# A graph layer's edge pass: 125-row gathers, columns in two groups of five, single rows on SyncE, the bias from node features in SBUF

## The chip, the cores and the metric

The kernel runs on one core of a Trainium2 chip. The core's engines are TensorE (PE: matmuls; PEld: its weight loads), VectorE (DVE), ScalarE (ACT), GpSimd (POOL) and SyncE (SP), which issues most of the plain transfers. Sixteen DMA engines move the data between HBM and the core's memory (SBUF, and PSUM for matmul results). The metric is device time in microseconds (us), as the median of several runs.

## The reference

One message-passing layer on 12500 nodes with 64 features each and 412500 edges (both directions of 200000 random edges, and a loop for every node), sorted by receiver. With `h = relu(layernorm(x))`, cut to what matters:

```python
msg_in = concat([h[src], h[dst], edge_attr], axis=-1)       # 412500 x 160
messages = swish(msg_in @ W1 + b1) @ W2 + b2                # 412500 x 64
att = softmax(swish(msg_in @ Wa1 + ba1) @ Wa2 + ba2, axis=0)  # over all edges
aggregated = segment_sum(messages * att, dst, 12500)
upd = concat([h, aggregated], axis=-1)
out = x + swish(upd @ Wu1 + bu1) @ Wu2 + bu2
```

Everything is float32.

## The kernel before, in words

**Tables by node.** The first layers of message and attention are linear in the three parts of `msg_in`. So a prologue normalizes the nodes and computes two tables of 128 numbers per node (64 for attention, 64 for messages): `ts_d` for senders and `tr_d` for receivers, both in HBM. The normalized features stay in SBUF, transposed, as `hT` (two nodes' 64 features stacked on 128 partitions, 49 x 128 columns), and go to HBM as `hT_d`, too.

**The edge pass.** Edges go in blocks of 125 (`EP`), eight blocks (`K`) to a group, 413 groups (`NG`). For each group `load(g)` starts two groups ahead (`AHEAD`):

- POOL gathers the senders' rows of `ts_d` by an indirect DMA per block (L513), 125 or 126 rows of 512 bytes into `gs`, from a pool of seven buffers (`gather`). Each block has 125 edges; with `WIDE` = 126 the blocks with odd j fetch a row more, into a partition that nobody reads.
- SP loads the receivers' windows of 32 rows (`wins`, L534, three buffers), and every fourth group (`NQ`) the edge features (`eo`, L524) and receivers' numbers (`dbs`, L527). DVE turns the numbers into a one-hot matrix (L538), and PE adds receivers' and edges' share in PSUM (`pe`, L542).

**Blocks by columns.** For some groups (`chosen`, before: every third) POOL gathers seven blocks only. For the eighth, SP loads the senders' numbers into `num` (L458) and DVE turns them into column numbers of `hT` (`places`, L467 to L473). ACT reads these into registers and copies one column at a time from `hT` to `cols` (L484), in six lots of up to 24 spread over three groups (`burst`, `SLOTS`). DVE masks the half that is meant (L547), and PE multiplies by the senders' weights into the same PSUM (L548).

**After the gather.** `begin(g)` adds gathered rows and PSUM on DVE (L553; a block by columns is copied, L555), and ACT takes the tanh (L556). `end(g)` forms messages and attention logits on DVE (L566 to L577). Softmax runs online, in batches of four groups. `by_node` (L620, L626), `project` (L637) and `put` (L651 to L658) sum the weighted messages by receiver into `sums` in SBUF, some groups behind.

**Tiles for the end.** The last stage needs two things by node tile: the update's bias, `h @ Wu1[:64] + bu1`, and `x + bu2`. They are made during groups 17 to 119, in 13 tiles (`NT`), and go to HBM (`bq_d`, `xb_d`). `node_bias` loads the features back from `hT_d` into `hb` (L329), sets a row of ones by a DVE memset (L327) and lets PE multiply by the weights with the bias as 65th row (L331); ACT copies the result (L348). `tile_rest` loads x into a buffer of the same pool (L366), adds `bu2` on DVE (L370) and stores (L371), all within one group.

**What sets the order.** The loop over g is written out by hand: `pin` keeps the order on an engine. Unpinned instructions (tile bias, DMAs) are placed by a scheduler. Each engine works its own instructions in order and waits on semaphores. DMAs of a kind take turns on eight semaphores: in the built program a DMA of SP (or a gather of POOL) waits for the landing of the eighth one before it.

Of the kernel before, what the change touches and what calls it, by code (L numbers as in the profile page):

```python
# [44 lines left out]
F32 = mybir.dt.float32  # L45
I32 = mybir.dt.int32
AF = mybir.ActivationFunctionType
ALU = mybir.AluOpType
AX = mybir.AxisListType
ENG = mybir.EngineType  # L50
# [3 lines left out]
P = 128  # L54
EP = 125
D = 64
DE = 32
U = 64
C = 2 * U
S1 = U + 1  # L60
K = 8
# [11 lines left out]

EVERY = 3
PHASE = 1
SLOTS = (((0, 24), (24, 24)), ((48, 24), (72, 12)), ((84, 24), (108, 17)))
ROUND = 12582912.0
WIDE = 126
EPS = 1e-5
# [4 lines left out]
PARTS = [("pair", 4 * C), ("we", C), ("bias", C), ("wu2h", 2 * D), ("wa2", U), ("bu2", D), ("w_bu", U),  # L84
         ("w2b", U), ("wu1a", U), ("wu2", D), ("ba2", 1)]
HALVED = 4
# [4 lines left out]
def gnn_kernel(ctx: ExitStack, tc: tile.TileContext, n_edges, x, src, src_row, dst, dst_row, first, edge,  # L91
# [33 lines left out]
    we, bias, wa2, bu2_r, ba2_c = (part[k] for k in ("we", "bias", "wa2", "bu2", "ba2"))  # L125
    w_bu = part["w_bu"][:D + 1]
    w2b = part["w2b"][:S1]
    wu1a, wu2 = part["wu1a"][:U], part["wu2"][:U]
# [206 lines left out]
def tile_bias(tc, c, first, v, work, ps, bus):  # L335

    nc = tc.nc
    m = min(NC, v["NB"] - c)
    if first:
        bus[c] = work.tile([U, P * NC], F32, name="bu", bufs=1)[:, :P * m]  # L340
    elif m <= 4:
        return
    i = 0 if first else 4
    n = min(4, m - i)
    pb = node_bias(tc, c + i, v, work, ps).rearrange("u b (h p) -> u h p b", h=2)
    to = bus[c].rearrange("u (h k p b) -> u k h p b", h=2, k=2, b=m // 2)
    for k in range(i // (m // 2), (i + n) // (m // 2)):
        nc.scalar.copy(to[:, k], pb[:, :, :, k * m // 2 - i:(k + 1) * m // 2 - i])  # L348
    if i + n == m:
        for h in range(2):  # L350
            nc.sync.dma_start(v["bq_d"][c // NC, h * U:(h + 1) * U, :P // 2 * m],
                              bus[c][:, h * P // 2 * m:(h + 1) * P // 2 * m])


def halves(ap, c, n, k, NB):

    return ap.rearrange("(h p b) d -> p h b d", h=2, b=NB)[:, :, c + k * n // 2:c + (k + 1) * n // 2, :]


def tile_rest(tc, c, v, work):  # L360

    nc = tc.nc
    n = min(NC, v["NB"] - c)
    xt = work.tile([P, 4, P], F32, name="hb").rearrange("p a b -> p (a b)")[:, :n * D]
    for k in range(2):
        nc.sync.dma_start(  # L366
            xt[k * P // 2:(k + 1) * P // 2].rearrange("p (h b d) -> p h b d", h=2, d=D),
            halves(v["x"], c, n, k, v["NB"]))
    xv = xt.rearrange("p (b d) -> p b d", d=D)
    nc.vector.tensor_tensor(xv, xv, v["bu2_r"][:, None, :].to_broadcast([P, n, D]), ALU.add)  # L370
    nc.sync.dma_start(v["xb_d"][c // NC, :, :n * D], xt)  # L371


def one_pass(tc, n_edges, v):
    nc = tc.nc
    NB, T, NG, NP, NT = (v[k] for k in ("NB", "T", "NG", "NP", "NT"))
    ident, iota_w, bj, dloc, src_full, base_sb, real, unreal, far, wrong = (
        v[k] for k in ("ident", "iota_w", "bj", "dloc", "src_full", "base_sb", "real", "unreal",
                       "far", "wrong"))
# [12 lines left out]
    with ExitStack() as ctx:  # L392
# [5 lines left out]
        stand = keep.tile([P, NH + 2 * W], F32, name="stand")  # L398
        base_lo = keep.tile([1, NG + 1], I32, name="base_lo")
        base_hi = keep.tile([1, NG + 1], I32, name="base_hi")  # L400
        nc.vector.memset(base_lo, 0)
# [34 lines left out]
        with tc.tile_pool(name="work2", bufs=2) as work2, \  # L436
                tc.tile_pool(name="small", bufs=3) as small, \
                tc.tile_pool(name="pre_ps", bufs=AHEAD + 1, space=PSUM) as pre_ps, \
                tc.tile_pool(name="one_ps", bufs=1, space=PSUM) as one_ps:
            pes, gss, lgs, ps_, psums, sps, pps, ees, mts, nums, cols = ({} for _ in range(11))  # L440

# [9 lines left out]

            chosen = {g for g in range(8, NG - 12) if g % EVERY == PHASE}

            def numbers(g):
                if g in chosen:
                    e = (g * K + K - 1) * EP
                    n = nums[g] = small.tile([P, EP], I32, name="num", bufs=2)
                    nc.sync.dma_start(n, bass.AP(tensor=v["src_row"].tensor,  # L458
                                                 offset=v["src_row"][:, e:].offset, ap=[[0, P], [1, EP]]))

            def places(g):
                if g not in chosen:
                    return
                n = nums[g]
                near = small.tile([1, EP], F32, name="near", bufs=1)
                to = small.tile([1, EP], I32, name="to", bufs=2)
                pin(nc.vector.tensor_scalar(to, n[0:1], 1, None, op0=ALU.logical_shift_right))  # L467
                m = NB // 2
                pin(nc.vector.tensor_scalar(near, to, 1.0 / m, 0.5 / m - 0.5, op0=ALU.mult, op1=ALU.add))
                pin(nc.vector.tensor_scalar(near, near, ROUND, None, op0=ALU.add))  # L470
                pin(nc.vector.tensor_scalar(near, near, ROUND, float(1 - m * P), op0=ALU.subtract, op1=ALU.mult))
                pin(nc.vector.scalar_tensor_tensor(to, to, float(P), near, op0=ALU.mult, op1=ALU.add))
                pin(nc.vector.tensor_scalar(n, n, 1, None, op0=ALU.bitwise_and))  # L473
                cols[g] = small.tile([P, EP], F32, name="cols", bufs=2), to

# [10 lines left out]
            def burst(g, k):  # L486
                for i in range(EVERY):
                    columns(g + 3 + i, *SLOTS[EVERY - 1 - i][k])

            at_sp, at_lo, at_hi, bus = {}, {}, {}, {}  # L490

# [12 lines left out]
            def load(g):  # L504

                t = g * K
                if g % NQ == 0:
                    registers(g, ENG.SP, at_sp)
                full = gather.tile([P, K, C], F32, name="gs")
                gs = gss[g] = full[:EP]  # L510
                for j in range(K - (g in chosen)):
                    rows = WIDE if j % 2 == 1 else EP
                    nc.gpsimd.indirect_dma_start(  # L513
                        out=full[:rows, j, :], out_offset=None, in_=ts_d[:, :],
                        in_offset=bass.IndirectOffsetOnAxis(ap=src_full[:rows, t + j:t + j + 1], axis=0))
                if g % NQ == 0:
# [16 lines left out]
                for r in range(2):  # L533
                    nc.sync.dma_start(win[r * R:(r + 1) * R, :, r, :],  # L534
                                      tr_w[bass.ds(at_sp[g], R), :, :])
                for h in range(2):
                    e = slice(h * E2 // 2, (h + 1) * E2 // 2)
                    pin(nc.vector.tensor_scalar(eo[:WR, e], db[:, e], bj[g // NQ % 2 * WR:(g // NQ % 2 + 1) * WR, g, h:h + 1], None,  # L538
                                                op0=ALU.is_equal))
# [10 lines left out]
            def begin(g):  # L550

                n = K - (g in chosen)
                pin(nc.vector.tensor_tensor(gss[g][:, :n, :], pes[g][:, :n, :], gss[g][:, :n, :], ALU.add))  # L553
                if n < K:
                    pin(nc.vector.tensor_copy(gss[g][:, n, :], pes[g][:, n, :]))  # L555
                pin(nc.scalar.activation(pes[g], gss[g], AF.Tanh))  # L556
# [161 lines left out]
            for g in range(NG):  # L718
# [18 lines left out]
                if g + AHEAD < NG:  # L737
                    load(g + AHEAD)
                numbers(g + EVERY + 4)
                places(g + EVERY + 3)  # L740
                if more:
# [20 lines left out]
                if g == min(40, NG):  # L762
                    pin(nc.vector.tensor_reduce(far[:, 1:2], dloc, AX.X, ALU.min, negate=True))
                if g == min(44, NG):

                    worst = small.tile([EP, 1], F32, name="worst", bufs=1)
                    pin(nc.vector.tensor_reduce(worst, far, AX.X, ALU.max))
                    worst_ps = one_ps.tile([P, 4, P], F32, name="mt")[:EP, 0, :EP]
                    pin(nc.tensor.transpose(worst_ps, worst.to_broadcast([EP, EP]), ident[:EP, :EP]))
                if g == min(45, NG):  # L770
                    pin(nc.vector.tensor_reduce(worst, worst_ps, AX.X, ALU.max))
                    pin(nc.vector.tensor_scalar(wrong, worst, 0.0, None, op0=ALU.is_gt))
                if g >= 16 and g // 8 - 2 < NT:
                    c = (g // 8 - 2) * NC
                    if g % 8 in (1, 5):
                        tile_bias(tc, c, g % 8 == 1, v, work2, one_ps, bus)
                    elif g % 8 == 3:
                        tile_rest(tc, c, v, work2)

# [273 lines left out]
def _laid_out(w):  # L1053
# [16 lines left out]
    part["ba2"][:] = w["ba2"]  # L1070
    part["w_bu"][:D + 1] = np.concatenate([w["Wu1"][:D], w["bu1"][None]])
    part["w2b"][:S1] = np.concatenate([w["W2"], w["b2"][None]])
    part["wu1a"][:U] = w["Wu1"][D:]
# [42 lines left out]
```

## Time and profile before

| | |
|---|---|
| median of 10 runs | 4599.79 us (4598.45 to 4601.67) |
| the profiled execution | 4599.87 us, span 4598.1 us |
| busy | POOL 3538.4 us, DVE 3355.3, PE 2388.4, ACT 2213.4 |
| gathers (L513) | 3173, first at 51.46 us, last at 4541.11 us |
| columns copied by ACT (L484) | 16375 |
| DMA, mean | 87 GB/s |

The profile is one execution, read on the core itself. The span reaches from the first to the last instruction; the profiled execution's own time has 1.8 us around it. A line of the groups reads: source line, engine, operation, tiles (out<-in), number of instructions | busy us, mean ns of one | idle us of the engine just before them, and what ended most of it. A line of the timeline reads: start, duration, engine, line, operation, and in brackets the idle time before it and what ended that. A line of the waits reads: who <- for whom: us in total, times, longest. A line of one source line reads: engine, operation, count, duration in ns (least, median, greatest), first and last start in us. A gather's duration on POOL is the time in which POOL issues it, not the time until its rows land. An engine name with q is its sequencer, which waits and issues DMAs.

### The profile page before, as it was taken

The numbers are of one execution on the slowest core, as the hardware profiler recorded it, in microseconds if no ns is written. First come the engines' busy times: TensorE is split into PE (matmuls) and PEld (weight loads), VectorE is DVE, ScalarE is ACT, GpSimd is POOL, SyncE is SP. The second block draws the span as 40 slices with busy tenths as digits, with TensorE's granted clock in tenths as the row PEclk, the third lists the DMA queues.
The fourth block names the chain that finished last, engine by engine and source line by source line (L and its number), as shares of the span: only waits on it lengthen the run. The fifth ranks groups of instructions, "written<-read, shape, count | busy, mean of one in ns | idle before, by whom it ended". The sixth has DMA issues, their size and how long they took to land. (4 is left out here: it accounts for less than half of the span.)

```text
span 4598.1 us, 81803 instructions
## 1 busy us (share of the span) xinstructions
PE 2388.4 (52%) x11509; PEld 1917.7 (42%) x11509; DVE 3355.3 (73%) x9768; ACT 2213.4 (48%) x17651; POOL 3538.4 (77%) x3198
## 2 busy tenths in 40 slices
PE   6455555555554554544555554555554555555455
PEld 4344444334444443434444444444443444444344
DVE  6767777777787776777777776777777777777777
ACT  3445545445554544544544444545545445445412
POOL 4777777777777777777777777777777777777775
PEclk8656666666666666566666655566666655556666
DMA  8333343343333333333333333333333333333333
GB/s 267 83 81 87 87 98 91 84 98 87 87 86 82 76 79 82 75 81 81 73 83 81 73 82 82 73 81 81 74 81 79 75 82 76 79 81 75 80 98 85
DMA packets 335625, 398.57 MB, mean 87 GB/s; under 512 B 170293, under 2 KB 266088, under 8 KB 334690
## 3 DMA queue, kind: packets, MB, share of 16 engines
q0 software_dynamic: 205168, 205.98, 19.5%
q1 hardware_dynamic: 128530, 177.64, 16.5%
q10 hardware_dynamic: 1376, 9.67, 0.5%
q14 instruction: 457, 3.74, 0.3%
q8 instruction: 94, 1.54, 0.1%
HBM read 365.34 MB, written 25.72 MB: 85 GB/s over the span
## 5 line engine op out<-in xcount | busy, mean ns | idle before, releaser
L513 POOL DMA_INDIRECT gs<-ts_d,src_sb x3173 | 3521.2, 1110 | 1018.5 <-issue 871.2
L542 PE MATMUL pe<-wins,eo 128*125 128x256 f32 x3304 | 1501.2, 630 | 1256.8 <-DVE eo L538 874.7
L484 ACT COPY cols<-hT 128x1 f32 x16375 | 1617.9, 187 | 749.0 <-issue 732.2
L542 PEld LDWEIGHTS pe<-wins,eo 128*125 128x125 f32 x3304 | 988.3, 316 | 1585.5 <-DVE eo L538 952.6
L553 DVE TENSOR_TENSOR gs<-pe,gs 125x1024 f32<-125x1024 f32 (+1 forms) x413 | 487.2, 1180 | 913.7 <-DMA gs<-ts_d,src_sb 878.4
L556 ACT ACTIVATE pe<-gs 125x1024 f32<-125x1024 f32 x413 | 424.1, 1027 | 1311.9 <-DVE gs L553 716.9
L620 DVE TENSOR_SCALAR wt<-iota_w,dloc,p 125x40 f32<-125x40 f32 x3304 | 749.4, 342 | 1.6
L626 PE MATMUL sp<-wt,acts 125*65 125x40 f32 x6608 | 634.3, 268 | 12.7 <-DVE wt L620 12.1
L626 PEld LDWEIGHTS sp<-wt,acts 125*65 125x65 f32 x6608 | 599.7, 184 | 18.2 <-DVE wt L620 16.7
L637 PEld LDWEIGHTS mt<-ss,w2u 65*128 65x128 f32 x826 | 211.6, 283 | 454.5 <-issue 359.2
L637 PE MATMUL mt<-ss,w2u 65*128 65x40 f32 x826 | 186.8, 320 | 367.1 <-DVE gm L603 358.8
L538 DVE TENSOR_SCALAR eo<-dbs,bj 64x250 f32<-64x250 int32 x826 | 300.7, 391 | 18.2 <-DMA dbs<-in_dst_row_dram 8.7
L596 PE MATMUL mt<-ident,mx 125*128 125x125 f32 x110 | 48.1, 437 | 507.5 <-DVE sums L655 430.7
L574 DVE TENSOR_TENSOR pe<-pe,w_all 125x512 f32<-125x512 f32 x413 | 288.7, 699 | 13.4
L572 DVE SCALAR_TENSOR_TENSOR pe<-pe,gs 125x512 f32<-125x512 f32 x413 | 286.7, 694 | 9.2
L566 DVE SCALAR_TENSOR_TENSOR acts<-pe,gs 125x512 f32<-125x512 f32 x413 | 283.3, 686 | 10.9 <-ACT pe L556 2.7
L577 DVE TENSOR_REDUCE lg<-pe 125x8 f32<-125x512 f32 x413 | 283.7, 687 | 9.4
L596 PEld LDWEIGHTS mt<-ident,mx 125*128 125x128 f32 x110 | 19.9, 181 | 518.9 <-issue 516.7
L658 DVE COPY stand<-nmax 64x40 f32 x826 | 183.5, 222 | 4.4
L655 DVE TENSOR_TENSOR sums<-sums,mt 64x40 f32 x606 | 114.3, 189 | 26.5 <-PE mt L637 21.1
L607 ACT ACTIVATE scale<-fall 128x1 f32<-128x1 f32 x110 | 22.2, 202 | 204.8 <-DVE fall L606 204.7
L651 DVE SCALAR_TENSOR_TENSOR sums<-sums,scale,mt 64x40 f32 x220 | 55.6, 253 | 72.4 <-PE mt L637 69.3
(125 smaller groups left out, 1102.1 us busy)
## 6 DMA issues: line engine op xcount, KB each, us to landing
eo<-in_edge_dram SPq DMA_DIRECT2D x103, 500.0 KB
dbs<-in_dst_row_dram SPq DMA_DIRECT2D x206, 250.0 KB
gs<-ts_d,src_sb POOLq DMA_INDIRECT x3173
wins<-tr_d SPq DMA_DIRECT2D x826, 32.0 KB
num<-in_src_row_dram SPq DMA_DIRECT2D x131, 62.5 KB
ts_d<-ts SPq DMA_DIRECT2D x5, 896.0 KB
tr_d<-tr ACTq DMA_DIRECT2D x5, 896.0 KB
hT_d<-hT ACTq DMA_DIRECT2D x1, 3136.0 KB
```

The source lines that it names most:

```text
L484: pin(nc.scalar.copy(to[:, first + i:first + i + 1], hT[:, bass.ds(regs[i], 1)]))
L513: nc.gpsimd.indirect_dma_start(out=full[:rows, j, :], out_offset=None, in_=ts_d[:, :], in_offset=bass.IndirectOffsetOnAxis(ap=src_full[:ro ...
L538: pin(nc.vector.tensor_scalar(eo[:WR, e], db[:, e], bj[g // NQ % 2 * WR:(g // NQ % 2 + 1) * WR, g, h:h + 1], None, op0=ALU.is_equal))
L542: pin(nc.tensor.matmul(pe[:, 2 * q:2 * q + 2, :], eo[:, q * EP:(q + 1) * EP], win[:, q // 2, :, :], start=True, stop=q < H - 1 or g not in ...
L553: pin(nc.vector.tensor_tensor(gss[g][:, :n, :], pes[g][:, :n, :], gss[g][:, :n, :], ALU.add))
L556: pin(nc.scalar.activation(pes[g], gss[g], AF.Tanh))
L572: pin(nc.vector.scalar_tensor_tensor(att, th[:, :, 0:U], 1.0, gs[:, :, 0:U], op0=ALU.add, op1=ALU.mult))
L574: pin(nc.vector.tensor_tensor(att, att, wa2[:EP, None, :].to_broadcast([EP, K, U]), ALU.mult))
L577: pin(nc.vector.tensor_reduce(lgs[s][:, k:k + K], att, AX.X, ALU.add))
L620: pin(nc.vector.tensor_scalar(wt[:, j, :], iota_w[:EP, j // H, :], dloc[:, g * K + j:g * K + j + 1], p[:, k + j:k + j + 1], op0=ALU.is_equ ...
L626: pin(nc.tensor.matmul(sp, acts[g % ACTS][:, j, :], wt[:, j, :], start=j == 0, stop=j == K - 1))
L637: pin(nc.tensor.matmul(pp, w2u.rearrange("s h u -> s (h u)"), sps.pop(g), start=True, stop=True))
```

## The change

- All gathers have 125 rows; `WIDE` goes.
- `chosen` takes two groups in five (g mod 5 = 1 or 4) instead of one in three. Their columns come in five lots of 24 (the last 29), at most one lot in each half of a group's pass.
- Every eighth group (8, 16, ... 408) leaves out one gather more. For this block SP reads the senders' numbers into registers and issues a transfer for each row of 512 bytes, 16 rows in each of the eight groups before it, into a tile of its own (`one_gs`); DVE adds the block by itself.
- The update's bias comes from `hT` in SBUF: PE multiplies two nodes' features at once by a weight matrix with two blocks (`w_bup`), and DVE adds `bu1` while it moves the result from PSUM. The loads of `hb` and the memset go. The instructions are pinned, and the store follows two groups later (`tile_bias_out`).
- `tile_rest` is split in three: x is asked for in one group, `bu2` is added three groups later, and the store follows three groups after that. x has a buffer of its own.

The core of the diff (`...` marks what is left out):

```diff
-EVERY = 3
-PHASE = 1
-SLOTS = (((0, 24), (24, 24)), ((48, 24), (72, 12)), ((84, 24), (108, 17)))
+LOTS = ((0, 24), (24, 24), (48, 24), (72, 24), (96, EP - 96))
+ROUNDS = 5
+SLOTS = {1: ((5, 1), (4, 0), (4, 1), (3, 0), (3, 1)), 4: ((5, 0), (5, 1), (4, 0), (4, 1), (3, 0))}
-WIDE = 126
+QUEUES = [(ENG.SP, 8, 0, 16)]
...
-    pb = node_bias(tc, c + i, v, work, ps).rearrange("u b (h p) -> u h p b", h=2)
+    pb = ps.tile([P, 4, P], F32, name="mt")[:, :n // 2, :]
+    pin(nc.tensor.matmul(pb, v["w_bup"], v["hT"][:, (c + i) // 2:(c + i + n) // 2, :], start=True, stop=True))
...
-        nc.scalar.copy(to[:, k], pb[:, :, :, k * m // 2 - i:(k + 1) * m // 2 - i])
...
+        pin(nc.vector.tensor_scalar(
+            to[:, k, :, :, at:at + 2 * q - 1:2],
+            pb[rows, (b - i) // 2:(b - i) // 2 + q, :].rearrange("u q (h p) -> u h p q", h=2),
+            v["bu1"][rows], None, op0=ALU.add))
...
-            chosen = {g for g in range(8, NG - 12) if g % EVERY == PHASE}
+            chosen = {g for g in range(8, NG - 12) if g % ROUNDS in SLOTS}
...
             def burst(g, k):
-                for i in range(EVERY):
-                    columns(g + 3 + i, *SLOTS[EVERY - 1 - i][k])
+                for i in (3, 4, 5):
+                    slots = SLOTS.get((g + i) % ROUNDS, ())
+                    if (i, k) in slots:
+                        columns(g + i, *LOTS[slots.index((i, k))])
...
+            def single(q, g):
+                if g < NG - 4:
+                    t = g * K + K - 1 - (g in chosen)
+                    rows_at[q, g] = small.tile([1, EP], I32, name=f"one_src{q}", bufs=2)
+                    nc.sync.dma_start(rows_at[q, g], v["src_row"][:, t * EP:(t + 1) * EP])
+            def rows(q, g):
...
+                loads, regs = nc.values_load_multi_w_load_instructions(
+                    rows_at[q, g][0:1, a:a + n], engines=[engine], min_val=0, max_val=NP - 1,
+                    skip_runtime_bounds_check_because=WHY)
+                for one in loads:
+                    pin(one)
+                for k in range(n):
+                    pin(dma[engine].dma_start(alone[g][a + k:a + k + 1, :], ts_d[bass.ds(regs[k], 1), :]))
...
-                for j in range(K - (g in chosen)):
-                    rows = WIDE if j % 2 == 1 else EP
+                for j in range(K - (g in chosen) - (g in alone)):
                     nc.gpsimd.indirect_dma_start(
-                        out=full[:rows, j, :], out_offset=None, in_=ts_d[:, :],
-                        in_offset=bass.IndirectOffsetOnAxis(ap=src_full[:rows, t + j:t + j + 1], axis=0))
+                        out=gs[:, j, :], out_offset=None, in_=ts_d[:, :],
+                        in_offset=bass.IndirectOffsetOnAxis(ap=src_sb[:, t + j:t + j + 1], axis=0))
...
+                for q in range(len(QUEUES)):
+                    if QUEUES[q][0] == ENG.SP:
+                        rows(q, g)
...
+                if g in alone:
+                    pin(nc.vector.tensor_tensor(gss[g][:, n, :], pes[g][:, n, :], alone.pop(g), ALU.add))
```

## The prediction

> **What bounds the kernel now.** I began with the page's busy shares and costliest groups. POOL is the busiest engine, at 77%, and one line is almost all of it.
>
> ```profile
> PE 2388.4 (52%) x11509; PEld 1917.7 (42%) x11509; DVE 3355.3 (73%) x9768; ACT 2213.4 (48%) x17651; POOL 3538.4 (77%) x3198
> ...
> L513 POOL DMA_INDIRECT gs<-ts_d,src_sb x3173 | 3521.2, 1110 | 1018.5 <-issue 871.2
> ```
>
> The reader is to see that POOL's missing 23% is no slack. 1018.5 us of idle time lie before the 3173 gathers; the waits put 871.2 us of it down to "issue" in 2859 pieces of at most 0.3 us, and 49.1 us to the start. That is 0.30 us before every gather, with nothing to wait for: a gather costs its duration plus 0.30. Second, the timeline of POOL in a middle stretch:
>
> ```profile
> 2061.14 1.27 POOL L513 DMA_INDIRECT gs<-ts_d,src_sb  x1 [0.30 <-issue]
> 2062.72 1.00 POOL L513 DMA_INDIRECT gs<-ts_d,src_sb  x1 [0.30 <-issue]
> 2064.02 1.21 POOL L513 DMA_INDIRECT gs<-ts_d,src_sb  x1 [0.31 <-issue]
> 2065.53 1.21 POOL L513 DMA_INDIRECT gs<-ts_d,src_sb  x1 [0.30 <-issue]
> 2067.04 0.99 POOL L513 DMA_INDIRECT gs<-ts_d,src_sb  x1 [0.30 <-issue]
> 2068.34 1.21 POOL L513 DMA_INDIRECT gs<-ts_d,src_sb  x1 [0.30 <-issue]
> 2069.86 1.00 POOL L513 DMA_INDIRECT gs<-ts_d,src_sb  x1 [0.30 <-DVE sums L655]
> ```
>
> There are two kinds of gather, 1.21 and 1.00 us, in turn, with two long ones side by side now and then. The code issues 125 rows for even j and 126 for odd j. A group with a column block stops at j = 6, so j = 6 and the next group's j = 0 stand together, both with 125 rows: that is the pair of long ones. The order from the first gather on fits everywhere: 1652 gathers of 125 rows start on average 1.517 us before their successor, 1520 of 126 rows (the last one has none) 1.305 us before theirs. 1652 x 1.517 + 1520 x 1.305 = 4489.7 us, which is the distance from the first gather (51.46) to the last one (4541.11). So POOL is the bound from end to end. Of the rest of the span, 51.5 us lie before it and 57.0 us after the last start.
>
> Third, the waits of DVE and of SP's queue, and the nearest thing to a one-row transfer that SP issues, by its line:
>
> ```profile
> DVE gs L553 <- DMA gs<-ts_d,src_sb: 878.4, 256, 18.4
> ...
> SPq L534 <- PE pe L542: 1238.0, 164, 14.3
> ...
> L180 SPq DMA_DIRECT2D base_sb<-in_first_dram x1: 307/307/307, 8.2 to 8.2; - x1
> L534 SPq DMA_DIRECT2D wins<-tr_d x826: 316/317/1672, 82.9 to 4496.2; - x166
> ```
>
> The consumers wait for gathers (878.4 us on DVE, 2.1 us in each of 413 groups of 4490/413 = 10.87 us), POOL hardly for them. While bias and x tiles are made (groups 17 to 119) DVE's add starts up to 27 us after a group's last gather, and even then POOL runs on, since it has seven buffers. SP mostly waits for PE to free a window buffer, so it is ahead.
>
> **The change part by part.**
>
> *125 rows in every gather.* The 126-row kind goes, and each gather that was one pays 1.517 - 1.305 = +0.212 us. The trace has the case of a 125-row gather behind another of 125 rows 131 times: 1.515 us. All after the change stand so; I take 1.517. The packet sizes on the gathers' queue say why: 46074 packets of 4096 bytes and 29554 of 512, which is 1652 x 15 + 1521 x 14 and 1652 x 5 + 1521 x 14. So 125 rows go out as 5 shares of 25 rows (three packets of 8 rows and one of 1), 126 as 14 shares of 9 (one of 8, one of 1). That ties the duration to the row count and not to a place in the group.
>
> *Fewer gathers.* Before, groups 8 to 400 with g mod 3 = 1 (131) have one block by columns. After, g mod 5 = 1 or 4 there: 157. In addition 51 groups (8, 16, ... 408) get one block as single rows. 3304 - 157 - 51 = 3096 gathers, 77 fewer.
>
> *The sum on POOL.* 3095 steps of 1.517 = 4695.1 us, and 2.8 us for the one long wait at the start (3.14 instead of 0.30 at 91 us), which stood in the other kind's mean: 4697.9, against 4489.7: +208.2. The last gather now has 125 rows: from its start to its landing the median is 3.40 us, against 2.66 for 126: +0.7 on the tail. Total +208.9. The profiled execution took 4599.87 us (1.77 more than its span; the median is 0.08 lower), so 4599.87 + 208.9 = 4808.8. Split: 77 fewer gathers at the old mean of 1.415 give -109; 3096 dearer ones at 1.517 - 1.415 give +316.
>
> The page DMA: Bandwidth & Descriptors of the Trainium skill, section Anatomy of one DMA, gives a fixed cost that scales with nothing plus bytes over a rate. By it, 125 and 126 rows should cost POOL nearly the same, the row count would drop out, and the sum would be 77 x 1.415 less, an estimate of 4491. The two kinds in the timeline, 0.21 us apart at under 1% of bytes, speak against it.
>
> *Columns in two groups of five.* ACT copies 157 x 125 = 19625 columns instead of 16375; 24 take 2.32 us in the timeline, so 3250 more cost 314 us. Lots stay 785 against 786, so their register loads stay. ACT goes from 2213 to about 2510 us in a longer span, 52%. A pass has at most 29 + 29 columns, 5.6 us, and about 1.2 us of register loads, in an 11.3 us group. DVE gets 26 more groups of L467 to L473 (1.58 us), L547 (0.34) and L555 (0.28), less 0.13 on L553: +54 us. PE 26 x 0.75. All is covered by POOL's 11.3 us per group; without that cover the 54 us on DVE would be the price.
>
> *Single rows on SyncE.* 51 x 125 = 6375 issues more on SP, each a register operation (0.037), a move (0.029) and the transfer. The shape is not in the trace; the nearest row is the one-row load at 0.307, bounds 0.3 and 0.58 (the longer L527 loads). So 0.374 each, 15.6 per group: 5.8 us, and 0.34 for the register load. SP's issues, moves and loads before come to 666 us, 1.6 per group: together 7.8 us of 11.3. Behind them on the queue wait the window, edge and receiver loads of the next group. Each transfer also waits for the landing of the eighth before it: eight issues are 3.0 us, window loads land in 1.94 (median), edge loads in 5.4, so some 2.4 us more every fourth group. SP may run over two groups ahead (three window buffers), some 22 us: the 6 us are hidden. DVE gets 51 more adds, about 0.28 (L555): 14 us. The rows are asked for in the eight groups before, so nobody should wait for them. Price on the path: 0; lower bound 0, since a shorter wait of the consumers does not speed POOL; upper bound in rival 2.
>
> *Bias from SBUF, x rows asked for earlier.* 50 loads of hb (0.606 us each on SP), 25 memsets (12.1 us on DVE) and 26 ACT copies (13.8 us) go. In their place DVE does 50 adds out of PSUM, 64x256, between L655 (0.19) and L574 (0.70); the nearest shape, L538, says 0.39: 20 us. DVE's waits on hb (50.6 + 28.1 us) go or shrink. All of that lay beside POOL, which never stopped there: 0. What is late next is the same gather as before. Net on DVE: 54 + 14 + 20 - 12 = +76 us, 3431 of 4807, 71%.
>
> **Rivals.** 1. *The long and the short kind follow something other than the row count*, odd j for instance, which the trace has only together with 126 rows. Then of the 3096 gathers 1464 stay short: 1632 x 1.517 + 1464 x 1.305 = 4386.3, 103 less than 4489.7: 4496, faster. For it: no 125-row gather with odd j exists before. Against: the packets, which differ as the row counts do. It decides against me if the mean step falls below 4490 / 3096 = 1.450, that is if over 31% of the gathers stay short.
>
> 2. *SP becomes the bound.* With 1.95 us of other work per group this needs (11.34 - 1.95) / 15.6 = 0.60 us per single row, or landings of more than 11.34 / (18 / 8) = 5 us. At 0.65 (the 0.58 row and its moves) a group takes 12.1 us; 400 of these with the 272 us around them: 5112. Against: 0.307 and 0.317 for small transfers, and landings of 1.94 us.
> [...]
>
> 3. *Consumers come late here and there*, for uneven groups of 6 to 8 gathers or rows on their way; POOL then runs out of buffers: 10 to 50 us more, 4820 to 4860. Against: it did not at 27 us of lag.
>
> **How the numbers follow.** My forecast 0.90, rival 1 0.04, rival 2 0.03, rival 3 0.03. 0.2% (9 us) is about what a measurement of this kernel can tell from no change. Slower: 0.90 + 0.03 + 0.03, less a little for something unnamed, 0.95; faster 0.04; same 0.01. The range starts at 4790, a step of 1.511, below any 125-row mean here, and reaches to 4860 to take in rival 3. Rivals 1 and 2 stay outside.
>
> **What would show it.** Right: POOL gathers x3096 of 1.21 us without short ones, 0.30 idle before each, and the last start near 4749. DVE's wait for gathers grows from 878 us, as 208 us of span bring only 76 of work. SP's single rows at about 0.31. Wrong: 1.00 us gathers among those of 125 rows; POOL waiting for DVE; DVE waiting for one_gs or wins at SP.

## The result, and the profile after

The changed kernel takes 4808.1 us (4806.5 to 4810.9), the kernel before 4599.7 us beside it: a ratio of 1.0454, 95% interval 1.0444 to 1.0463. It is slower by 208 us, and the forecast was 4809. The profiled execution took 4808.78 us with a span of 4807.1.

The page of the changed kernel, busy shares and the groups that answer to those shown of before:

```profile
PE 2482.8 (52%) x11561; PEld 1984.3 (41%) x11561; DVE 3514.6 (73%) x10052; ACT 2499.4 (52%) x20875; POOL 3769.7 (78%) x3121
...
L571 POOL DMA_INDIRECT gs<-ts_d,src_sb x3096 | 3752.5, 1212 | 996.7 <-issue 884.9
```

77 gathers fewer than before, and 231 us more of POOL's time in them, since the mean went from 1110 to 1212 ns. The timeline of POOL in the same middle stretch, and its last gather:

```profile
2060.23 1.21 POOL L571 DMA_INDIRECT gs<-ts_d,src_sb  x1 [0.30 <-issue]
2061.74 1.21 POOL L571 DMA_INDIRECT gs<-ts_d,src_sb  x1 [0.30 <-issue]
...
4750.38 1.21 POOL L571 DMA_INDIRECT gs<-ts_d,src_sb  x1 [0.30 <-issue]
```

The short gathers of 1.00 us are gone. Before each gather stand the same 0.30 us with nothing to wait for, so POOL sets the time from end to end, as before: (4750.4 - 51.6) / 3095 = 1.518 us per step. The waits of POOL, DVE and PE, and of SP's queue:

```profile
POOL gs L571 <- issue: 884.9, 2900, 0.3
DVE gs L614 <- DMA gs<-ts_d,src_sb: 851.6, 318, 7.3
DVE bu L357 <- PE mt L348: 120.2, 25, 10.2
PE pe L603 <- DMA wins<-tr_d: 116.8, 27, 11.2
DVE eo L599 <- DMA dbs<-in_dst_row_dram: 61.5, 7, 18.8
...
SPq L592 <- PE pe L603: 212.9, 109, 11.0
```

The wait of 1238.0 us on SP's queue, the sign that SP was ahead, has shrunk to 212.9: the single rows have eaten most of SP's lead, and PE and DVE now wait for window and receiver loads here and there. None of this reaches POOL: after its first gather it waits longer than 0.4 us only three times, all before 95 us, and 13 of its 3095 steps are over 1.7 us (3.22 at most), 11 of them in the first 1300 us.

### The profile page after: what moved, and what is told of

It is laid out like the page before. It is cut to its first block, busy times and chain, and to the rows that moved or that the text cites. A ratio compares the mean times of both kernels' runs of the same rounds, so it can differ in the third digit from the quotient of the medians.

```text
span 4807.1 us, 108404 instructions
## 1 busy us (share of the span) xinstructions
PE 2482.8 (52%) x11561; PEld 1984.3 (41%) x11561; DVE 3514.6 (73%) x10052; ACT 2499.4 (52%) x20875; POOL 3769.7 (78%) x3121
## 5 line engine op out<-in xcount | busy, mean ns | idle before, releaser
L571 POOL DMA_INDIRECT gs<-ts_d,src_sb x3096 | 3752.5, 1212 | 996.7 <-issue 884.9
L504 ACT COPY cols<-hT 128x1 f32 x19625 | 1922.2, 187 | 962.5 <-issue 931.4
L603 PE MATMUL pe<-wins,eo 128*125 128x256 f32 x3304 | 1547.4, 642 | 1468.5 <-DVE eo L599 1079.1
L614 DVE TENSOR_TENSOR gs<-pe,gs 125x1024 f32<-125x1024 f32 (+2 forms) x413 | 477.4, 1156 | 873.0 <-DMA gs<-ts_d,src_sb 851.6
L683 DVE TENSOR_SCALAR wt<-iota_w,dloc,p 125x40 f32<-125x40 f32 x3304 | 782.6, 367 | 1.2
L689 PE MATMUL sp<-wt,acts 125*65 125x40 f32 x6608 | 671.6, 275 | 11.1 <-DVE wt L683 10.3
L689 PEld LDWEIGHTS sp<-wt,acts 125*65 125x65 f32 x6608 | 631.9, 191 | 20.9 <-DVE wt L683 16.3
L599 DVE TENSOR_SCALAR eo<-dbs,bj 64x250 f32<-64x250 int32 x826 | 301.0, 394 | 70.8 <-DMA dbs<-in_dst_row_dram 61.5
L721 DVE COPY stand<-nmax 64x40 f32 x826 | 215.5, 261 | 3.2
L357 DVE TENSOR_SCALAR bu<-mt,w_all 64x256 f32<-64x256 f32 (+1 forms) x50 | 23.9, 478 | 120.6 <-PE mt L348 120.2
```

Source lines behind the costliest of these rows:

```text
L504: pin(nc.scalar.copy(to[:, first + i:first + i + 1], hT[:, bass.ds(regs[i], 1)]))
L571: nc.gpsimd.indirect_dma_start(out=gs[:, j, :], out_offset=None, in_=ts_d[:, :], in_offset=bass.IndirectOffsetOnAxis(ap=src_sb[:, t + j:t ...
L603: pin(nc.tensor.matmul(pe[:, 2 * q:2 * q + 2, :], eo[:, q * EP:(q + 1) * EP], win[:, q // 2, :, :], start=True, stop=q < H - 1 or g not in ...
L683: pin(nc.vector.tensor_scalar(wt[:, j, :], iota_w[:EP, j // H, :], dloc[:, g * K + j:g * K + j + 1], p[:, k + j:k + j + 1], op0=ALU.is_equ ...
L689: pin(nc.tensor.matmul(sp, acts[g % ACTS][:, j, :], wt[:, j, :], start=j == 0, stop=j == K - 1))
```

## The experiments

Each kernel was timed beside the kernel before on the same chip, in three rounds; a row of the table gives both. E1 to e4 ran together on another chip than the rest. On that one the kernel before itself took 5390 us instead of 4600, so those four are compared only with each other, and what set that chip apart is taken up at the end.

| run | rows per gather | columns | single rows | gathers | us | before beside it | ratio (95%) |
|---|---|---|---|---|---|---|---|
| before | 125, odd j 126 | 1 in 3 | no | 3173 | 4599.7 | | |
| after | 125 | 2 in 5 | yes | 3096 | 4808.1 | 4599.7 | 1.0454 (1.0444 to 1.0463) |
| e1 | 125 | 1 in 3 | no | 3173 | 4931.0 | 5390.1 | 0.9143 (0.9117 to 0.9170) |
| e2 | 125, even j 126 | 1 in 3 | no | 3173 | 5478.5 | 5390.1 | 1.0172 (1.0135 to 1.0210) |
| e3 | 125, odd j 126 | 2 in 5 | yes | 3096 | 6161.0 | 5390.1 | 1.1421 (1.1387 to 1.1455) |
| e4 | 125 | 2 in 5 | no | 3147 | 4892.7 | 5390.1 | 0.9071 (0.9045 to 0.9096) |
| e5 | as e3 | 2 in 5 | yes | 3096 | 4500.8 | 4598.2 | 0.9785 (0.9769 to 0.9801) |
| e6 | as e2 | 1 in 3 | no | 3173 | 4573.4 | 4598.2 | 0.9945 (0.9928 to 0.9961) |
| e7 | 126 | 2 in 5 | yes | 3096 | 4325.3 | 4598.2 | 0.9405 (0.9389 to 0.9420) |
| e8 | 128 | 2 in 5 | yes | 3096 | 4318.3 | 4598.2 | 0.9392 (0.9376 to 0.9407) |
| e9 | 128 | 2 in 5 | no | 3147 | 4052.8 | 4599.4 | 0.8812 (0.8797 to 0.8826) |
| e10 | 128 | 1 in 3 | no | 3173 | 4087.3 | 4599.4 | 0.8887 (0.8872 to 0.8902) |
| e11 | 128 | 1 in 5 | no | 3226 | 4147.6 | 4599.4 | 0.9018 (0.9003 to 0.9033) |
| e12 | 128 | 1 in 2 | no | 3108 | 4467.4 | 4598.9 | 0.9715 (0.9699 to 0.9732) |

In e4 and e9 to e12 the eighth block of groups 8, 16, ... is gathered again instead of read as single rows; all kernels compute the whole layer.

### Row count alone and each part alone, first try (e1 to e4)

My theory: the row count sets a gather's time, and the rest of the change is worth its 77 gathers. The rivals: the place in the group (odd or even j) sets it; or the single rows on SP cost something.

```diff
 # e1 and e2, in the kernel before
-                    rows = WIDE if j % 2 == 1 else EP
+                    rows = EP                              # e1
+                    rows = WIDE if j % 2 == 0 else EP      # e2
 # e3, in the changed kernel
-                gs = gss[g] = gather.tile([P, K, C], F32, name="gs")[:EP]
+                full = gather.tile([P, K, C], F32, name="gs")
+                gs = gss[g] = full[:EP]
...
+                    wide = 126 if j % 2 == 1 else EP
-                        out=gs[:, j, :], out_offset=None, in_=ts_d[:, :],
-                        in_offset=bass.IndirectOffsetOnAxis(ap=src_sb[:, t + j:t + j + 1], axis=0))
+                        out=full[:wide, j, :], out_offset=None, in_=ts_d[:, :],
+                        in_offset=bass.IndirectOffsetOnAxis(ap=v["src_full"][:wide, t + j:t + j + 1], axis=0))
 # e4, in the changed kernel
-QUEUES = [(ENG.SP, 8, 0, 16)]
+QUEUES = []
```

> The kernel before with 125 rows in every gather; nothing else changes. Theory (the row count sets POOL's step, and POOL is the bound): 3172 steps of 1.517 us instead of 1652 of 1.517 and 1520 of 1.305, so 4600 + 1520 x 0.212 = about 4922 us, and no gather of 1.00 us is left. Rival 1 (the place in the group, odd j, sets it): the 1.00 us gathers stay where j is odd, time unchanged at 4600.

> The kernel before with 126 rows at even j and 125 at odd j, the other way round. Theory (row count): 1652 gathers are now short and 1520 long, 131 more short ones than before: 4600 - 131 x 0.212 = about 4572 us, and the gathers at even j show 1.00 us. Rival 1 (odd j is short whatever its rows): odd j stays at 1.00 us and even j at 1.21, time unchanged at 4600.

> The changed kernel with one part undone: 126 rows at odd j again. Theory (the row count is all of the loss, and the rest of the change is worth its 77 fewer gathers): 1632 steps of 1.517 and 1463 of 1.305, so 4808 - 1463 x 0.213 = about 4497 us, 2.2% under the kernel before. Rival 3 (the single rows or the uneven groups hold the consumers up once POOL is quicker): above 4520 us, with POOL waiting for buffers.

> The changed kernel without single rows on SyncE: POOL gathers these 51 blocks, too. Theory (the 6375 transfers on SP are covered, and only POOL's count matters): 51 more steps of 1.517 us, 4808 + 77 = about 4885 us. Rival 2 in its mild form (the single rows cost something on the path themselves): less than 77 us more, since their cost goes as well.

The two kernels with 125 rows alone came within 9 us of the number expected (4931.0 and 4892.7), although the kernel before lost 790 us on this chip. Their difference, 38.2 us, is that of e4's 26 gathers fewer: 26 x 1.518 = 39.5. So at this pace the columns in two of five and the new bias are worth their gathers and nothing else. E2 and e3 lost 900 and 1660 us against what was expected, and settle nothing on the row count; they were run again on another chip.

### The row count against the place in the group (e5, e6)

> The changed kernel with 126 rows at odd j again, repeated. In e1 to e4 the kernel before itself took 5390 us instead of 4600, and e3's trace shows ScalarE's register operations at 0.7 us instead of 0.037 in 1693 places and POOL standing still for them. Theory: that was the chip; where the kernel before takes 4600 us, this one takes about 4497 us (1632 steps of 1.517, 1463 of 1.305). Rival: the mixture of 126-row gathers and single rows is at fault itself, and it stays above 4800 us even where the kernel before takes 4600.

> The kernel before with 126 rows at even j, repeated. Theory (row count): 131 more short gathers than before, 28 us less than the kernel before, about 4572 us where that takes 4600. Rival 1 (odd j is short by its place): no difference from the kernel before.

The timeline of POOL in e6, the kernel before with the extra row at even j:

```profile
2063.53 1.21 POOL L513 DMA_INDIRECT gs<-ts_d,src_sb  x1 [0.30 <-issue]
2065.04 0.99 POOL L513 DMA_INDIRECT gs<-ts_d,src_sb  x1 [0.30 <-issue]
2066.34 1.21 POOL L513 DMA_INDIRECT gs<-ts_d,src_sb  x1 [0.30 <-issue]
```

The short gathers have moved with the extra row: in the whole trace the 1652 gathers at even j have a median of 0.997 us and the 1521 at odd j 1.210, where before it was 1.209 at even j and 0.996 at odd j. The row count sets the time, the place does not. E6 has 1652 short gathers and 1521 long ones, before it was the other way round; the 131 that are short in its place make it 24.8 us faster, 0.19 us each, against 0.21 between the two kinds. E5 splits the change: with 126 rows at odd j back in place, the rest of it brings 97 us (4500.8 against 4598.2). So taking the 126th row away costs 4808.1 - 4500.8 = 307 us over 1464 gathers, 0.210 us each.

### More of the quick kind: 126 and 128 rows in every gather (e7, e8)

With every gather short, POOL's pace becomes quick enough to see what stands behind it. E7 and e8 are e3's edit with `wide = 126` and `wide = P` (128); the rows past 125 are read by nobody.

> The changed kernel with 126 rows in every gather. Theory: 3095 steps of 1.305 us, 4039 us, and 110 us around them: about 4150 us if the consumers keep up; they need some 9.3 us per group (11.34 less 2.06 us of DVE's waits for gathers) against 9.8 that POOL then takes, so up to 4300 us where they fall behind. Rival: a 126-row gather is short only because a 125-row one stands before it; then the steps show about 1.5 us and the time stays near 4800 us.

> The changed kernel with 128 rows in every gather: 16 shares of 8 rows by the pattern of the packets (125 rows: 5 shares of 25; 126 rows: 14 shares of 9). If the step goes by rows per share, as 25 -> 1.21 us and 9 -> 1.00 us of duration suggest (0.013 us per row), it is about 0.99 us, the step 1.29, and the time 4100 to 4300 us. Rival: the step goes by the number of shares or rows beyond 126, and the gathers take longer than 1.00 us.

Without waits, 3095 steps of 0.996 + 0.30 us and of 0.944 + 0.30, with 108 us before and behind them, would give 4119 and 3958 us. The runs gave 4325.3 and 4318.3, above the 4300 us that were expected at most, and hardly different from each other, so something else sets the pace. The group line of POOL, the leading waits and a wait of SP's queue in e8:

```profile
L573 POOL DMA_INDIRECT gs<-ts_d,src_sb x3096 | 2934.3, 948 | 1279.6 <-issue 1120.4
...
POOL gs L573 <- issue: 1120.4, 2765, 9.2
PE pe L605 <- DMA wins<-tr_d: 747.4, 215, 9.6
...
DVE to L487 <- DMA num<-in_src_row_dram: 304.5, 97, 8.1
...
DVE gs L616 <- DMA gs<-ts_d,src_sb: 9.3, 39, 0.6
...
SPq L594 <- PE pe L605: 8.9, 21, 2.8
```

A gather of 128 rows takes 0.95 us, yet a step is (4215.4 - 51.3) / 3095 = 1.345 us on average and not 1.25: POOL's waits now reach 9.2 us. DVE waits for gathers 9.3 us in all instead of 851.6: gathers are early now, and window loads late. The timelines of POOL and of SP's queue show how one stop comes about:

```profile
3014.32 0.94 POOL L573 DMA_INDIRECT gs<-ts_d,src_sb  x1 [0.30 <-issue]
3020.53 0.94 POOL L573 DMA_INDIRECT gs<-ts_d,src_sb  x1 [5.27 <-issue]
```

```profile
3008.93 0.85 SPq L594 DMA_DIRECT2D wins<-tr_d  x2
...
3011.65 6.03 SPq L548 DMA_DIRECT2D one_gs<-ts_d  x13
...
3019.01 0.86 SPq L594 DMA_DIRECT2D wins<-tr_d  x2
3021.09 6.47 SPq L548 DMA_DIRECT2D one_gs<-ts_d  x16
3027.81 0.86 SPq L594 DMA_DIRECT2D wins<-tr_d  x2
```

SP has hardly a gap left: it waits only 8.9 us for PE's window matmul to free a buffer (212.9 in after, 1238.0 before). Between two pairs of window loads stand 16 single rows of about 0.4 us each, and POOL, out of buffers, stands still from 3015.3 to 3020.5. A group takes 10.1 us, (4215.4 - 51.3) / 413.

### The same without single rows (e9), and the kernel before with 128 rows (e10)

If SP's single rows are the bound of e8, taking them out must make it faster although POOL gets 51 gathers more. If something else stands behind it (DVE at 79%, or ACT), it must not.

```diff
 # e9, in e8
-QUEUES = [(ENG.SP, 8, 0, 16)]
+QUEUES = []
 # e10, in the kernel before
-                    rows = WIDE if j % 2 == 1 else EP
+                    rows = P
```

> e8 without the single rows on SyncE. In e8 POOL's gathers take 0.94 us (step 1.247), yet the time is 4318 us, not 3095 x 1.247 + 110 = 3970: POOL stands still for its buffers, PE waits 747 us for window loads and DVE 304 us for num, both queued behind the single rows on SP. Theory (with quick gathers SP is the bound, rival 2): without them 3146 steps of 1.247 and 110 make 4033 us at the least, and the waits for wins and num go, so well below e8, 4030 to 4200 us. Rival (DVE is the bound at 79% busy, the SP waits are only seen first): no more than 1% below e8, since 51 more gathers come and only 14 us of DVE work go.

> The kernel before with 128 rows in every gather: no single rows, columns for one group in three, the bias from HBM. 3172 steps of 1.247 and 110 us: 4066 us at the least. Theory (SP's single rows held e7 and e8 up, the rest of the change matters little): below e8's 4318 us, and near e9, by 33 us of POOL if that is the bound there. Rival (the other parts of the change, bias from SBUF and columns, are worth something once gathers are quick): over 1.5% above e9, with waits on hb.

The lines of e9 that answer to those of e8:

```profile
PE 2429.1 (60%) x11561; PEld 1951.7 (48%) x11561; DVE 3381.5 (83%) x10001; ACT 2497.0 (62%) x20875; POOL 3002.7 (74%) x3172
...
L573 POOL DMA_INDIRECT gs<-ts_d,src_sb x3147 | 2985.5, 949 | 1008.5 <-issue 886.1
...
POOL gs L573 <- issue: 886.1, 2908, 0.3
...
DVE gs L616 <- DMA gs<-ts_d,src_sb: 311.7, 160, 6.2
```

51 gathers more, and 265 us less. POOL's waits are back at 0.3 us, the waits for windows are down to 22.4 us, those for senders' numbers are gone, and DVE waits for gathers again: the single rows were e8's bound. POOL's step is (3995.4 - 51.1) / 3146 = 1.254 us. The 51 gathers that the single rows save are worth 51 x 1.254 = 64 us, so at this pace they cost 265 + 64 = 329.

E10 is the kernel before with one edit, 128 rows in every gather: 4087.3 us, 11.1% less than 4599.4. E9 is 34.5 us below it, with 26 gathers fewer: 26 x 1.254 = 32.6. E10 is thus 0.9% above e9 and not over 1.5%, so with quick gathers, too, the rest of the change is worth little beyond its gathers.

### How far the columns carry (e11, e12)

```diff
 # e11, in e9
-SLOTS = {1: ((5, 1), (4, 0), (4, 1), (3, 0), (3, 1)), 4: ((5, 0), (5, 1), (4, 0), (4, 1), (3, 0))}
+SLOTS = {1: ((5, 1), (4, 0), (4, 1), (3, 0), (3, 1))}
 # e12, in e9
-ROUNDS = 5
-SLOTS = {1: ((5, 1), (4, 0), (4, 1), (3, 0), (3, 1)), 4: ((5, 0), (5, 1), (4, 0), (4, 1), (3, 0))}
+ROUNDS = 2
+SLOTS = {1: ((5, 0), (5, 1), (4, 0), (4, 1), (3, 0))}
```

> e9 with columns for one group in five instead of two: 78 more gathers, 9750 fewer columns on ScalarE, and 78 x 2.1 = 164 us less on DVE. If POOL is the bound in e9: 78 x 1.247 = 97 us above e9, 4130 us at the least. If DVE or ScalarE is the bound there: below e9, by up to 164 us.

> The kernel of e9 (128-row gathers, no single rows), with columns taken in every second group of edges instead of in two of five: 196 chosen groups instead of 157, so 39 gathers fewer (3108 instead of 3147), paid with 39 x 125 = 4875 more column copies on ScalarE and 39 more sets of column operations on VectorE. Theory A: POOL's steps of 1.25 us still set the time, as in e9 and e11, where 79 gathers more cost 94.8 us. Then 39 gathers fewer give 39 x 1.247 = 49 us: 4052.8 - 49 = 4004 us, and POOL hardly waits for buffers. Theory B: a consumer is now the bound. VectorE rises by 39 x 2.1 = 82 us over its 3381 (to some 3463, 86%) and ScalarE by 4875 x 0.099 = 480 us over 2497; VectorE waited only 311.7 us for gathers in e9. Then the time does not fall (4045 or more) and POOL's idle time before gathers grows by over 40 us beyond 0.3 us a gather.

With one group in five the 79 gathers more cost 94.8 us, 1.20 us each: POOL's pace. With every second group the kernel loses 414.5 us against e9, so theory B has the right side, but it had no number for the size. Page and waits of e12:

```profile
PE 2548.0 (57%) x11639; PEld 2029.8 (45%) x11639; DVE 3468.4 (78%) x10313; ACT 2969.1 (66%) x25750; POOL 2961.7 (66%) x3133
...
L573 POOL DMA_INDIRECT gs<-ts_d,src_sb x3108 | 2944.5, 947 | 1431.1 <-issue 1261.6
...
POOL gs L573 <- issue: 1261.6, 2717, 6.9
ACT cols L504 <- issue: 1154.1, 1290, 1.7
...
PE mt L702 <- ACT ss L697: 666.0, 194, 4.9
...
DVE acts L631 <- ACT pe L621: 290.1, 190, 3.4
...
ACT pe L621 <- DVE gs L616: 76.7, 18, 9.1
```

DVE's and ACT's busy times are what was worked out (3463 and 2977 expected). What the expectation left out is in the second line of the waits: the time in which ACT reads column numbers into registers before each lot is no busy time. It rose from 919.3 us in e9 to 1154.1. Busy and reading together, ACT is at 2969.1 + 1154.1 = 4123 of 4466 us, against 3416 of 4055 in e9. Its wait for DVE before the tanh fell from 229.3 to 76.7 us. PE now waits 666.0 us for ACT (2.9 in e9) and DVE 290.1 for its tanh (6.4 in e9), while DVE's wait for gathers fell from 311.7 to 4.2 us. So ACT became the bound: its 4123 us alone are more than the 4053 that e9 takes. That its columns stand ahead of the tanh in its order would explain why e12 takes 4467 and not some 4123; it was not tested. E9 is the fastest of the kernels that were run.

## Why the prediction was right

- **The bound and the sum.** "POOL is the bound from end to end" held, and with it the sum: steps of 1.518 against 1.517, last start 4750.4 against 4749, 56.7 us behind it against 57.7. The last start came 1 us later than forecast and the end 1 us sooner after it; that the sum met the profiled execution (4808.8) to the tenth of a us is luck. The forecast's group of 11.34 us should read 4697.9 / 413 = 11.37, on which nothing hangs. The two terms of the split can be checked by e5: its 4500.8 is the forecast sum with 1464 gathers left short, for which 4497 was expected.
- **Rival 1 (the kind follows odd j)** is refuted by e6, where the short gathers follow the extra row to even j, and by e7, where all are short.
- **The shares.** The packets of the gathers' queue are 46440 of 4096 bytes and 15480 of 512, 3096 x 15 and 3096 x 5, so five shares of 25 rows in each gather. In e8 there are 49536 of 4096 bytes and none of 512: 16 shares of 8 rows. The Trainium skill, DMA: Bandwidth & Descriptors, section Why a DMA increments its semaphore by 16 and not by 1, states that the number of engines is the largest up to 16 that divides the size of the slowest dimension on both sides, here the rows; the packets agree for 125 (5), 126 (14) and 128 (16). The step had the packet sizes "say why" 125 rows take longer. That is not shown: they tell how the rows are divided, not which part of it costs POOL time. The section Anatomy of one DMA gives its fixed cost for a DMA up to its completion and puts most of it down to the receipt of the write; it has no figure for the time that POOL is held, so the estimate of 4491 asked of the page what it does not give. In before, gathers landed 3.40 us (125 rows) and 2.66 us (126) after their start, and POOL's own time per gather was 1.21, 1.00 and 0.944 us for 125, 126 and 128 rows: the row count drops out of neither, and the measurement decides.
- **Columns on ACT.** Busy 2499.4 us against 2510; no pass has more than 24 + 29 columns, not 29 + 29. "Lots stay 785 against 786, so their register loads stay" failed: the number of loads stays, but the lots are larger, and a load takes longer the more numbers it reads (median 0.79 us for a lot of 12, 1.50 for 24, 2.0 for 29). ACT's idle time before columns, which is where the loads show, went from 732.2 to 931.4 us. Harmless here, as forecast; e12 shows where it ends, and that the loads count, which the step named (1.2 us a pass) and then left out of the total.
- **Single rows on SP: priced right at zero, for a wrong reason in part.** The step "0.374 each, 15.6 per group: 5.8 us, and 0.34 for the register load" gave SP 7.8 us a group and some 2.4 more every fourth. One line of each instruction in the trace after (count, duration least, median and greatest in ns, first and last start in us):

```profile
L548 SPq DMA_DIRECT2D one_gs<-ts_d x6375: 224/228/374, 88.0 to 4645.0; - x200
L542 SPq TENSOR_LOAD <-one_src x408: 973/1167/2157, 86.1 to 4638.6; - x136
```

  The transfer itself is cheaper than forecast (0.228, with 0.037 and 0.029 before it), but about 0.12 us of idle time stands around these three instructions, so that 16 of them take 6.6 us (median), 0.41 each, and the register load is three times the forecast. The wait for the eighth landing hardly counts: a row landed in 1.36 us (median), and eight of them take 3.3. E8, where SP has hardly a gap, gives the true demand: 10.1 us a group, not 7.8. At POOL's 11.4 us that still fits, by 1.3 us instead of 3.5.
- **Rival 2 (SP becomes the bound)** did not come at this pace, but its mechanism is real: it needs POOL to take less than 10.1 us for a group, and in e7 and e8 it would have (3095 steps of 1.296 and 1.244 us are 9.7 and 9.3 us a group). At 11.4 us a group, 0.41 us for a single row stayed under the 0.60 that rival 2 needs, and window loads landed in 2.65 us (median; 1.94 before), not in 5. The wait of SP for PE, 1238.0 us before and 212.9 after, was the sign of it.
- **DVE's work was mis-sized.** "Net on DVE: +76 us, 3431" is measured as +159, 3514.6. Of the 83 us too few, 65 are in two lines that the change does not touch, whose single operations became longer: the weights (782.6 us against 749.4) and a copy of 64x40 (L721, 215.5 against 183.5 on L658); the last section shows when that happens. The sign "DVE's wait for gathers grows from 878 us" failed with it: it is 851.6, since DVE is busy 83 us more than forecast and new waits of 120.2 us for the bias matmul and 61.5 us for receivers' numbers took the room. Beside POOL none of it cost anything.
- **Rival 3 (consumers come late)** did not come: after its start POOL waited for no buffer (see its waits and its 13 long steps above).

## What to carry to other kernels

When one queue of equal pieces sets the time, cost a change by the count of the pieces and by the duration of each kind in the trace: removing 77 of 3173 gathers is worth 97 us (e5), and losing one spare row in half of them costs 307. A row that nobody needs can be the cheaper choice; here 128 rows in place of 125 and 126 take 11% off the kernel before by one edit (e10). Work that is "free" on another engine's queue is free only at the pace at which it was looked at: the single rows cost nothing at 11.4 us a group and 329 us at e9's pace, and idle time that an engine spends reading registers counts as use when you ask what more it can take.

## What the runs showed of the hardware

**Some small DVE operations last until the gather beside them ends.** The same instruction, 125x40, forms the weights in each kernel; the group lines of after, before and e7:

```profile
L683 DVE TENSOR_SCALAR wt<-iota_w,dloc,p 125x40 f32<-125x40 f32 x3304 | 782.6, 367 | 1.2
```

```profile
L620 DVE TENSOR_SCALAR wt<-iota_w,dloc,p 125x40 f32<-125x40 f32 x3304 | 749.4, 342 | 1.6
```

```profile
L685 DVE TENSOR_SCALAR wt<-iota_w,dloc,p 125x40 f32<-125x40 f32 x3304 | 740.9, 312 | 1.2
```

365 to 367 ns in all three kernels with 125 rows alone (after, e1, e4), 342 to 344 in the mixed ones on an undisturbed chip (before, e5, e6), 312 to 321 with 126 or 128 alone. The median hardly moves (296 in after, 295 before, 294 in e9); the mean is raised by some that take up to 0.75 us. The 125x512 additions keep a median of 699 or 700 ns in all of them. The traces show which operations are long: in after all 823 weight operations of over 0.4 us end within 0.1 us of the end of a gather on POOL. Those that start 0.4 to 0.9 us after a gather's start take 514 ns on average, the others 295. The one-hot of L599, a TENSOR_SCALAR like the weights, takes 565 ns there and 345 elsewhere. In e9 all 273 long ones end so, too, but a gather of 128 rows ends 0.26 us sooner, and those that start from 0.4 to 0.9 us take 354 ns. One case in after, a gather on POOL and the copy of 64x40 on DVE, which has a median of 0.18 us:

```profile
2057.20 1.21 POOL L571 DMA_INDIRECT gs<-ts_d,src_sb  x1 [0.30 <-issue]
2057.92 0.47 DVE L721 COPY stand<-nmax 64x40 f32 x1
```

Both end at 2058.4. After a long copy the next DVE operation starts 0.49 us after the copy's start instead of 0.18 (median), so this time is lost; after a long weight operation it starts 0.21 us later as after a short one, so there the longer duration is not all lost time. What DVE and POOL share in the later part of a gather, no run here shows.

**A step between 9 and 8 rows a share.** 0.996 us for 14 shares of 9 rows (e7), 0.944 for 16 shares of 8 (e8), 1.209 for 5 shares of 25 (after). Three points do not fix the law: share count, rows per share and packets differ together (the queue's packets of all sizes are 48, 32 and 80 per gather).

**One chip on which register work was slow.** The waits of ACT on the columns' register loads in e1 and in e2, which ran on it in the same set:

```profile
ACT cols L484 <- issue: 828.9, 1210, 2.0
```

```profile
ACT cols L484 <- issue: 2280.0, 3658, 2.2
```

The two kernels do the same work on ACT. In e2 1785 of ACT's register operations took over 0.3 us, 1218 us together, in e3 1693, 1132 us together, in e1 170 and in e4 176; in the traces from other chips none did. SP had slow ones, too: 1497 in e3, 1008 us together, against 148 in e2 and about 60 in e1 and e4. Beyond its 0.31 us before each gather POOL stood still for 848 us in e2 and 1613 us in e3, nearly all that the two lost. In e3 PE waited 2279.1 us for window loads, so there SP's slow operations are in the path as well; how much of a loss is ACT's and how much SP's was not separated. Why it hit the kernels that mix 125 and 126 rows, and hardly those with 125 alone, stays open.
